# Tracing a band's combine straight behind its deformable products, with later depthwise taps tied behind its first VectorE operation

## The chip, the cores and the metric

The kernel runs on one core of a Trainium2 chip, in one launch. The metric is the device time of that launch in microseconds. A core has a matrix engine (TensorE, PE in the profile, with its weight loads as PEld), VectorE (DVE), ScalarE (ACT), GpSimd (POOL) and SyncE (SP), which run side by side, each through its own list of instructions in a fixed order, and hand results to one another by semaphores. Transfers are issued from the lists of SP, ACT and POOL.

## What is computed

Two layers over 32 images of 96 channels and 56 x 56 pixels, in float32. The first is an inverted bottleneck with a squeeze-and-excite branch, the second a block with channel and spatial attention, a plain and a deformable 3 x 3 convolution, a gate that mixes them, a normalisation over the batch, and a residual.

```
# layer 0, per image
h = silu(bn1(conv1x1(x, w1)))            # 96 -> 576 channels
h = silu(bn2(depthwise3x3(h, w2)))       # nine taps per channel
s = sigmoid(se_w2 @ silu(se_w1 @ mean(h)))
x = x + bn3(conv1x1(h * s, w3))          # 576 -> 96
# layer 1
y      = x * channel_attention(|rfft2(x)|) * spatial_attention(x)
aux    = concat(y, coords, resized mean |rfft2(y)|)
offset = conv3x3(aux, off_w)
gate   = sigmoid(dg2 @ relu(conv3x3(aux, dg1_w)))
y_base = conv3x3(y, base_w) + base_b
y_def  = einsum(bilinear samples of y at pixel + offset, def_w) + def_b
z      = (1 - gate) * y_base + gate * y_def
out    = relu(batch_norm(z over batch and pixels) + x)
```

## The kernel before

**Tiling.** An image is worked in seven bands of eight rows, 448 pixels each: 224 bands (L1088). A band is sampled in two halves h of 224 pixels. For a half, `weights_load` brings two tiles of interpolation weights, wc and wr, from memory; `weights` (L710) multiplies them on VectorE; `sample_tiles` (L739) multiplies blocks of y with the result on TensorE, in a first group of 12 matmul records and a second of 16; ScalarE copies the samples to v (L743) and packs them (L750); `deform` (L758) multiplies v with the deformable weights into the PSUM tile pd, in 14 records for a half. There is one pd buffer, shared by a band's halves, so a band's first product needs the band before to have been read out of it.

**Combining.** `combine` reads pd on VectorE in L797 (z = pd + def_b - y_base), mixes it with the gate in L798 and L799, and takes statistics of z in L800. L797 is the only reader of pd. `join` (L1063) calls `combine` and puts the store of z seven slots later.

**Three streams side by side.** While the bands of image b are sampled, the expansion and depthwise part of image b+2 (`hidden`) and the projection, transforms and attention of image b+1 (`attend`) are traced between them: `pump` (L1027) counts a slot, advances both streams in proportion, and runs what stands in the list `later` for that slot. A band has 17 slots. An image's `hidden` stream has 40 steps over 119 slots, and is started at the sixth band (j = 5, L1124). An image has nine units of hidden channels, each with nine depthwise taps on VectorE over a tile acch: the first a multiplication (L260), the other eight a multiply-add each (L262); then ScalarE applies silu (L222) and stores the unit. There are two acch and two hp buffers (hp holds the expanded channels). For the first two images alone, three of the taps run on TensorE and L258 adds them.

**What sets the order.** The order in which an engine issues is not the order of the text. A scheduler plays the program through beforehand: whenever an engine is free it takes, of the instructions whose inputs and buffers are ready in its model, the one traced first. An instruction that is traced later but ready sooner so goes ahead. On the chip that order is fixed. Three things restrain it. SP keeps the traced order (L1368). `keep_in_program_order` ties one instruction behind the instruction that was traced just before it on its engine; `weights` uses it (L710). `issue_after(i)` ties everything that a block traces on i's engine behind i. These ties are of issue order alone.

**Where the pieces are traced.** In band m, half 0: the first sampling group, three pumps, then the waiting ends: `end_half` of the band n = m - 1, half 1 (`deform` and, two slots later by way of `later`, `join`). Directly behind the ends stand `weights` for the half (m, 1) and the transposes for that half. Then come the second sampling group, four pumps and the pack. In half 1 the same is done with `end_half` of (m, 0), which has no join.

Of the kernel before, what the change touches and what calls it, by code (L numbers as in the profile page):

```python
# [1 line left out]

# [8 lines left out]
ALU = mybir.AluOpType  # L11
# [5 lines left out]
C, H, W = 96, 56, 56  # L17
# [18 lines left out]
BW = NBW  # L36
# [81 lines left out]
def bank(p):  # L118
    return p["mm"].tile([128, 512], FP, name="mm")
# [33 lines left out]
def expand(nc, p, xts, unit):  # L153


    w = p["w0"]
    ch, half = unit
    h1 = p["hp"][p["n_hp"] % len(p["hp"])]
    p["n_hp"] += 1
    p["h1"] = h1  # L160
    inv, sh = w["inv1"][:, ch : ch + 1], w["sh1"][:, ch : ch + 1]
    w1 = w["w1"][:, ch * 128 : min(HID, ch * 128 + 128)]

    def piece(parts, row0, rows):

        pt = bank(p)
        for p0, hf in parts:
            r0 = row0 - 1 + hf
            nc.tensor.matmul(pt[p0 : p0 + w1.shape[1], : rows * W], w1, xts[hf][:, r0 * W : (r0 + rows) * W],  # L169
                             start=True, stop=True)  # L170
        lo = parts[0][0]
        hi = parts[-1][0] + w1.shape[1]
        nc.scalar.activation(h1[lo:hi, row0 : row0 + rows, 1 : 1 + W],  # L173
                             pt[lo:hi, : rows * W].rearrange("p (h w) -> p h w", h=rows), AF.Silu,
                             bias=sh[lo:hi], scale=inv[lo:hi])

    if half is None:
        nc.vector.memset(h1[:64, 0, :], 0.0)
        nc.vector.memset(h1[64:, HH + 1, :], 0.0)
        for r in range(1, HH + 1, ER):  # L180
            piece([(0, 0), (64, 1)], r, ER)
            yield
        piece([(0, 0)], HH + 1, 1)
        piece([(64, 1)], 0, 1)
        yield
    else:
        r = 1 - half
        for rows in (ER + 1, ER, ER, ER):
            piece([(0, half)], r, rows)
            r += rows  # L190
            yield
# [12 lines left out]
def hidden(tc, p, x, xn, h2d, pooled, defer):  # L204


    nc = tc.nc
    w = p["w0"]

    def rows_of(x, half):  # L210
        xt = p["xt"].tile([C, (HH + 1) * W], FP, name="xt")
        r0 = half * (HH - 1)
        nc.sync.dma_start(xt, x[:, r0 : r0 + HH + 1].rearrange("c h w -> c (h w)"))
        return xt

    xts = p.pop("xts", None) or [rows_of(x, 0), rows_of(x, 1)]
    for _ in expand(nc, p, xts, UNITS[0]):
        yield
    def finish(u, acc):
        ch = UNITS[u][0]  # L220
        flat = acc.rearrange("p h w -> p (h w)")
        tc.keep_in_program_order(nc.scalar.activation(  # L222
            flat, flat, AF.Silu, bias=w["sh2"][:, ch : ch + 1], scale=w["inv2"][:, ch : ch + 1], accum_out=pooled[:, u : u + 1]))
        nc.scalar.dma_start(h2d[u], flat)

    before = None
    for u, (ch, half) in enumerate(UNITS):
        h1 = p["h1"]
        more = expand(nc, p, xts, UNITS[u + 1]) if u + 1 < len(UNITS) else iter(())
        if xn is not None and u in (5, 8):  # L230

            p.setdefault("xts", []).append(rows_of(xn, int(u == 8)))
        acc = p["acch"].tile([128, HH, W], FP, name="acch")

        rows_of_tap = lambda dy: (int(half == 0 and dy == 0), HH - int(half == 1 and dy == 2))
        diag = p.get("diag")
        taps = [k for k in (4, 0, 1, 2, 3, 5, 6, 7, 8) if diag is None or k not in TPE]
        parts = []
        if diag is not None:
            for r0 in range(0, HH, ER):  # L240
                pt = bank(p)[:, :EW].rearrange("p (h w) -> p h w", h=ER)
                for i, k in enumerate(TPE):
                    dy, dx = divmod(k, 3)
                    lo, hi = rows_of_tap(dy)
                    lo, hi = max(r0, lo), min(r0 + ER, hi)
                    nc.tensor.matmul(pt[:, lo - r0 : hi - r0], diag[:, ch, i], h1[:, dy + lo : dy + hi, dx : dx + W],
                                     start=(i == 0), stop=(i == len(TPE) - 1))
                parts.append((slice(r0, r0 + ER), pt))
            next(more, None)
            yield  # L250
        for n, k in enumerate(taps):
            dy, dx = divmod(k, 3)
            lo, hi = rows_of_tap(dy)
            win = h1[:, dy + lo : dy + hi, dx : dx + W]
            wk = w["w2"][:, ch, k : k + 1]
            if n == 0:
                for rs, pt in parts:
                    nc.vector.scalar_tensor_tensor(acc[:, rs], win[:, rs], wk, pt, ALU.mult, ALU.add)  # L258
                if not parts:
                    nc.vector.tensor_scalar(acc, win, wk, None, ALU.mult)  # L260
            else:
                nc.vector.scalar_tensor_tensor(acc[:, lo:hi], win, wk, acc[:, lo:hi], ALU.mult, ALU.add)  # L262
            if n % 2:
                if n == 3 and before:
                    finish(u - 1, before)
                next(more, None)
                yield
        for _ in more:
            pass
        before = acc  # L270
    defer(lambda: finish(len(UNITS) - 1, before))


def sigmoid(nc, out, src, bias):
# [478 lines left out]
def deform(nc, p, pd, v, h):  # L753

    out = pd[:C, :BW].rearrange("c (q w) -> c q w", q=RB)[:, :, h * W // 2 : (h + 1) * W // 2]
    for k in range(KA):
        ks = slice(0, 128 if k else C)
        nc.tensor.matmul(out.rearrange("c q (t x) -> c t q x", x=TS), p["w"]["def"][ks, k],  # L758
                         v[ks, k].rearrange("c t s (r x) -> c t (s r) x", r=TS),
                         start=(k == 0), stop=(k == KA - 1))  # L760
# [33 lines left out]
def combine(nc, p, j, pd, yb, gate, st):  # L794

    z = p["q2"].tile([C, BW], FP, name="z")
    nc.vector.scalar_tensor_tensor(z, pd[:C, :BW], p["w"]["cv"]("def_b"), yb, ALU.add, ALU.subtract)  # L797
    nc.vector.scalar_tensor_tensor(z, gate, 1.0, z, ALU.add, ALU.mult)  # L798
    nc.vector.scalar_tensor_tensor(z, z, 0.5, yb, ALU.mult, ALU.add)  # L799
    nc.vector.bn_stats(st[:, j], z)  # L800
    return z
# [152 lines left out]
def layers(tc, a, dp, x1d, zd, stats, far):  # L954
# [6 lines left out]
    nc = tc.nc  # L961
    B = x1d.shape[0]
    with ExitStack() as ctx:
        p = {"tc": tc, "dp": ctx.enter_context(tc.tile_pool(name="l1d", bufs=3, space=DRAM))}
# [11 lines left out]
        def first(b):  # L976
            if b >= B:
                return iter(())
            h2d = p["dp"].tile([len(UNITS), 128, HB], FP, name="h2d")
            pooled = p["pl"].tile([128, len(UNITS)], FP, name="pooled")  # L980
            held[b] = h2d, pooled
            return hidden(tc, p, a["x"][b], a["x"][b + 1] if b + 1 < B else None, h2d, pooled, lambda end: later.append((slot + 3, end)))
# [7 lines left out]
        streams, later = [], []  # L990
        slot = 0
# [68 lines left out]
        def store(b, j, z):  # L1060
            nc.gpsimd.dma_start(zd[b][:, j * BW : (j + 1) * BW], z)

        def join(n, pd, gate, st):  # L1063
            b, j = bands[n]
            z = combine(nc, p, j, pd, ybs[n], gate, st)
            later.append((slot + 7, lambda: store(b, j, z)))
            if j == NBD - 1:
                nc.vector.bn_aggr(stats[:, b], st)

        def end_half(n, h, v, gate, st):  # L1070
            if h == 0:
                pds[n] = p["pd"].tile([128, 512], FP, name="pd")
            deform(nc, p, pds[n], v, h)
            if h:
                pd = pds.pop(n)
                later.append((slot + 2, lambda: join(n, pd, gate, st)))

        ends, pds = [], {}

# [41 lines left out]
        for n, (b, j) in enumerate(bands):  # L1121
            if j == 0:
                st = p["st"].tile([C, NBD, 6], FP, name="st")
# [7 lines left out]
            for h in range(2):  # L1131
# [20 lines left out]
                if h == 0:  # L1152
                    if n % 2 == 0:
                        gates.extend(gates_of(nc, p, hids[n // 2]))
                    gate = gates.pop(0)
# [361 lines left out]
```

## Time and profile before

| | |
|---|---|
| median of three runs | 9030.57 us (9027.98 to 9034.88) |
| profiled execution | 9059.03 us, its span 9057.2 us |
| PE busy (matmuls) | 8175.3 us, 90% of the span |
| DVE busy | 7184.4 us, 79% |
| ACT busy | 5393.5 us, 60% |
| POOL busy | 2902.8 us, 32% |
| mean granted TensorE clock | 0.939 of full |
| depthwise multiply-adds L262 | 2250, mean 1981 ns, 4456.4 us |
| first taps L260 | 270, mean 1084 ns |
| weight products L710 | 448, mean 1265 ns |
| combine L797, L798, L799, L800 | 224 each, mean 679, 876, 679, 618 ns |
| deformable products L758 | 6272 records, 1468.8 us |

Busy time is the time in which an engine had an instruction running. A line of the waits view names an engine with the line that it wanted to run, whom it waited for, and then the total in us, how often, and the longest. A line of the timeline has the start and duration in us, engine, line, operation, written and read tiles, and how many were merged; a bracket holds the idle time just before it and what ended it. TensorE's clock is given as a share of full speed (PEclk). The last stage, the normalisation from about 8775 us on, has no matmuls.

### The profile page before, as it was taken

How to read it: one execution, taken by the hardware profiler on the slowest of the kernel's cores; microseconds unless marked ns; L12 is line 12 of the kernel's file. 1: busy time of each engine (PE TensorE's matmuls, PEld its weight loads, DVE VectorE, ACT ScalarE, POOL GpSimd, SP SyncE). 2: the span in 40 equal slices, each digit the busy share in tenths (PEclk: the TensorE clock that was granted, in tenths of full speed). 3: DMA queues.
4: the chain of work that ended last, by engine and by line, in shares of the span. 5: the costliest groups of instructions: out<-in, count | busy, mean ns of one | idle time of the engine just before them, and what ended most of it. 6: DMA issues, size and time to landing. Idle time of an engine off the chain costs nothing. (4 is left out here: it accounts for less than half of the span.)

```text
span 9057.2 us, 137476 instructions
## 1 busy us (share of the span) xinstructions
PE 8175.3 (90%) x52406; PEld 5193.5 (57%) x52406; DVE 7184.4 (79%) x6629; ACT 5393.5 (60%) x10486; POOL 2902.8 (32%) x2800
## 2 busy tenths in 40 slices
PE   5889999999999999999999999999999999999960
PEld 3456565665656566565656656565665655566640
DVE  7688888888888888888888888888888888888333
ACT  2356665666666666666666666666666666666553
POOL 0233333333333333333333333333333333333210
PEclk9889999999999999999999999999999999999985
DMA  2356666666666666666666666666666666666669
GB/s 82 108 142 160 163 169 165 157 154 153 163 166 171 166 157 147 158 165 164 172 161 154 159 157 168 165 174 161 154 154 160 165 166 172 166 156 144 144 188 416
DMA packets 1068758, 1486.48 MB, mean 164 GB/s; under 512 B 590191, under 2 KB 839839, under 8 KB 1055807
## 3 DMA queue, kind: packets, MB, share of 16 engines
q1 hardware_dynamic: 858995, 985.20, 46.4%
q10 hardware_dynamic: 153803, 329.80, 10.2%
q0 software_dynamic: 55296, 162.60, 6.7%
q8 instruction: 420, 6.88, 0.4%
q14 instruction: 244, 1.99, 0.1%
HBM read 1064.29 MB, written 412.65 MB: 163 GB/s over the span
## 5 line engine op out<-in xcount | busy, mean ns | idle before, releaser
L262 DVE SCALAR_TENSOR_TENSOR acch<-hp,w,acch 128x1512 f32<-128x1512 f32 (+1 forms) x2250 | 4456.4, 1981 | 141.4 <-ACT hp L173 103.8
L615 PE MATMUL mm<-yp,c_jointW 104*128 104x448 f32 x4032 | 1679.6, 568 | 10.1 <-DMA yp<-fqd 10.1
L758 PE MATMUL pd<-v,c_def 128*96 128x224 f32 (+1 forms) x6272 | 1468.8, 382 | 142.7 <-DVE z L797 115.6
L721 POOL COPY ybl<-yp 96x448 f32<-96x448 f32 x896 | 1048.3, 1198 | 1204.9 <-PE mm L725 1204.8
L758 PEld LDWEIGHTS pd<-v,c_def 128*96 128x96 f32 (+1 forms) x6272 | 1062.2, 176 | 449.8 <-issue 116.9
L615 PEld LDWEIGHTS mm<-yp,c_jointW 104*128 104x128 f32 x4032 | 776.6, 196 | 784.2 <-issue 747.4
L743 ACT COPY v<-mm 96x288 f32<-96x288 f32 (+1 forms) x2688 | 1004.3, 441 | 156.0 <-PE mm L739 109.3
L169 PE MATMUL mm<-xt,w 96*128 96x392 f32 (+3 forms) x2688 | 1058.5, 527 | 35.3 <-DMA xt<-in_x 33.1
L739 PE MATMUL mm<-wc,yt 64*96 64x144 f32 x12544 | 1056.9, 300 | 20.8 <-DVE sq L379 6.7
L739 PEld LDWEIGHTS mm<-wc,yt 64*96 64x96 f32 x12544 | 834.2, 164 | 317.3 <-issue 199.1
L173 ACT ACTIVATE hp<-mm,sh,inv 128x392 f32<-128x392 f32 (+2 forms) x1216 | 810.7, 673 | 344.8 <-PE mm L169 290.5
L710 DVE TENSOR_TENSOR wc<-wc,wr 128x1008 f32<-128x1008 f32 x448 | 566.6, 1265 | 412.5 <-DMA wr<-hd 385.1
L644 PE MATMUL mm<-yp,c_base0W 96*64 96x224 f32 x8064 | 830.1, 358 | 5.7 <-ACT hp L173 5.7
L329 PE MATMUL mm<-hq,w3s 128*96 128x392 f32 x2048 | 749.7, 510 | 63.6 <-DMA hq<-h2d 62.2
L672 POOL DMA_DIRECT2D od<-at x224 | 186.7, 834 | 1908.3 <-DVE at L664 1292.6
L750 ACT COPY v<-v 32x448 f32<-32x448 f32 x1344 | 755.1, 562 | 29.7
L727 ACT COPY yt<-mm 128x384 f32<-128x384 f32 (+1 forms) x896 | 353.9, 439 | 700.7 <-PE mm L725 699.0
L644 PEld LDWEIGHTS mm<-yp,c_base0W 96*64 96x64 f32 x8064 | 555.2, 135 | 282.7 <-issue 61.0
L635 ACT ACTIVATE hid<-mm,c_dg1b 50x448 f32<-50x448 f32 x224 | 140.8, 628 | 868.4 <-PE mm L615 858.4
L476 POOL TENSOR_TENSOR o<-o,xc 96x392 f32<-96x392 f32 x256 | 376.2, 1470 | 806.2 <-ACT o L339 804.2
L222 ACT ACTIVATE acch<-acch,sh,inv 128x1568 f32<-128x1568 f32 x288 | 488.4, 1696 | 202.8 <-DVE acch L262 176.5
L329 PEld LDWEIGHTS mm<-hq,w3s 128*96 128x96 f32 x2048 | 323.0, 166 | 395.2 <-issue 367.5
(194 smaller groups left out, 9325.3 us busy)
## 6 DMA issues: line engine op xcount, KB each, us to landing
h2d<-acch ACTq DMA_DIRECT2D x288, 784.0 KB
wc<-hd SPq DMA_DIRECT2D x896, 252.0 KB
wr<-hd SPq DMA_DIRECT2D x448, 504.0 KB
hq<-h2d SPq DMA_DIRECT2D x128, 980.0 KB
hq<-h2d SPq DMA_DIRECT2D x128, 784.0 KB
hq<-x1d SPq DMA_DIRECT2D x768, 98.0 KB
ht<-od SPq DMA_DIRECT2D x224, 252.0 KB
hd<-ho ACTq DMA_DIRECT2D x224, 252.0 KB
```

Of the source, the lines that this page charges most:

```text
L169: nc.tensor.matmul(pt[p0 : p0 + w1.shape[1], : rows * W], w1, xts[hf][:, r0 * W : (r0 + rows) * W], start=True, stop=True)
L173: nc.scalar.activation(h1[lo:hi, row0 : row0 + rows, 1 : 1 + W], pt[lo:hi, : rows * W].rearrange("p (h w) -> p h w", h=rows), AF.Silu, bia ...
L262: nc.vector.scalar_tensor_tensor(acc[:, lo:hi], win, wk, acc[:, lo:hi], ALU.mult, ALU.add)
L329: nc.tensor.matmul(pts[half][:C, :EW], w3s[:, ch], hq, start=(i == 0), stop=False)
L615: nc.tensor.matmul(view, weights[:, k], yp[:channels, r0 : r0 + RB, dx + PD - 1 : dx + PD - 1 + W], start=(k == 0), stop=(k == NTAP - 1))
L644: nc.tensor.matmul(pb[i * BC : (i + 1) * BC, : BW // 2].rearrange("p (h w) -> p h w", h=RB // 2), w["base"][:, k], yp[:C, r0 + i * RB // 2 ...
L710: p["tc"].keep_in_program_order(nc.vector.tensor_tensor(wc, wc, wr, ALU.mult))
L721: nc.gpsimd.tensor_copy(yb[:, :, s], blocks)
L739: nc.tensor.matmul(pt[k][:C, (t - lo) * KP : (t - lo + 1) * KP], yt[ps, t], s[ps, t * KP : (t + 1) * KP], start=True, stop=True)
L743: nc.scalar.copy(v[:C, :, lo:hi, k].rearrange("c k t p -> c t k p"), pt[k][:C, : (hi - lo) * KP].rearrange("c (t k p) -> c t k p", t=hi - ...
L750: nc.scalar.copy(v[C:, 1 + 2 * i : 3 + 2 * i], v[i * QC : (i + 1) * QC, KA:])
L758: nc.tensor.matmul(out.rearrange("c q (t x) -> c t q x", x=TS), p["w"]["def"][ks, k], v[ks, k].rearrange("c t s (r x) -> c t (s r) x", r=T ...
```

## The change

`end_half` calls `join` at once instead of putting it into `later` for two slots on. `combine` keeps its first instruction, L797, under the name "urgent". In `hidden`, every multiply-add of the depthwise part that is traced from then on is tied behind the latest such instruction. The first tap of a unit as it stands in the main loop (L260) is not inside such a block. Nothing is computed differently, and no instruction is added or removed.

```diff
@@ hidden
             if n == 0:
-                for rs, pt in parts:
-                    nc.vector.scalar_tensor_tensor(acc[:, rs], win[:, rs], wk, pt, ALU.mult, ALU.add)
+                with behind(p):
+                    for rs, pt in parts:
+                        nc.vector.scalar_tensor_tensor(acc[:, rs], win[:, rs], wk, pt, ALU.mult, ALU.add)
                 if not parts:
                     nc.vector.tensor_scalar(acc, win, wk, None, ALU.mult)
             else:
-                nc.vector.scalar_tensor_tensor(acc[:, lo:hi], win, wk, acc[:, lo:hi], ALU.mult, ALU.add)
+                with behind(p):
+                    nc.vector.scalar_tensor_tensor(acc[:, lo:hi], win, wk, acc[:, lo:hi], ALU.mult, ALU.add)
...
+def behind(p):
+    return p["tc"].issue_after(p["urgent"]) if "urgent" in p else nullcontext()
...
@@ combine
-    nc.vector.scalar_tensor_tensor(z, pd[:C, :BW], p["w"]["cv"]("def_b"), yb, ALU.add, ALU.subtract)
+    p["urgent"] = nc.vector.scalar_tensor_tensor(z, pd[:C, :BW], p["w"]["cv"]("def_b"), yb, ALU.add, ALU.subtract).ins
...
@@ end_half
-                later.append((slot + 2, lambda: join(n, pd, gate, st)))
+                join(n, pd, gate, st)
```

## The prediction

> **What bounds the kernel now.** I read the page first. TensorE is busy for 90% of the span, and in nearly all of the 40 slices for nine tenths or more; VectorE for 79%. The chain that ended last names only the closing stage without matmuls, so it says nothing of the bands.
>
> ```profile
> span 9057.2 us, 137476 instructions
> PE 8175.3 (90%) x52406; PEld 5193.5 (57%) x52406; DVE 7184.4 (79%) x6629; ACT 5393.5 (60%) x10486; POOL 2902.8 (32%) x2800
> PEclk9889999999999999999999999999999999999985
> L758 PE MATMUL pd<-v,c_def 128*96 128x224 f32 (+1 forms) x6272 | 1468.8, 382 | 142.7 <-DVE z L797 115.6
> ```
>
> So TensorE's idle time is what can be won or lost. Second, the waits of TensorE: the longest is for L797, the reader of pd; the others are small and also mostly for VectorE.
>
> ```profile
> PE pd L758 <- DVE z L797: 115.6, 26, 6.1
> PE acc L440 <- DVE m_fy L437: 72.8, 30, 5.6
> PE acc L440 <- DVE m_fe L437: 71.1, 31, 2.5
> PE mm L725 <- DVE at L664: 57.2, 28, 5.7
> ```
>
> Third, where the L797 waits lie. Over all 224 bands I took, from the instruction rows in order of time, the end of a band's last L758 record, the start of its L797 and the next L758. An idle TensorE of more than 1.5 us before that next product occurs 29 times, 124.2 us in all (the waits view puts some of it to other lines), and every one is at the last band of an image, j = 6. One of them, TensorE and then VectorE:
>
> ```profile
> 3687.09 2.81 PE L758 MATMUL pd<-v,c_def 96*96 96x224 f32 x14
> 3689.74 0.74 PE L725 MATMUL mm<-c_ident,ybl 96*128 96x96 f32 x7
> 3690.41 1.23 PE L739 MATMUL mm<-wc,yt 64*96 64x144 f32 x16
> ...
> 3693.25 0.90 PE L739 MATMUL mm<-wc,yt 64*96 64x144 f32 x12
> 3694.09 0.93 PE L169 MATMUL mm<-xt,w 96*128 96x392 f32 x2
> 3698.67 1.06 PE L758 MATMUL pd<-v,c_def 96*96 96x224 f32 x2 [3.66 <-DVE z L797]
> ...
> 3700.17 4.43 PE L758 MATMUL pd<-v,c_def 128*96 128x224 f32 x12
> ```
>
> ```profile
> 3684.42 1.19 DVE L710 TENSOR_TENSOR wc<-wc,wr 128x1008 f32<-128x1008 f32 x1
> ...
> 3691.64 6.26 DVE L262 SCALAR_TENSOR_TENSOR acch<-hp,w,acch 128x1568 f32<-128x1568 f32 x3
> 3697.94 0.68 DVE L797 SCALAR_TENSOR_TENSOR z<-pd,c_cvec,yb 96x448 f32<-96x448 f32 x1
> ```
>
> pd was done at 3689.8, three taps ran on VectorE, L797 began 8.1 us later. The product after it takes 4.43 us for 12 records against 2.81 for 14, because the clock fell:
>
> ```profile
> 3692.00:3695.00 3.00, 3.00 (x20) 1.37 (x18) 2.96 (x2) 2.98 (x6) 3.00 (x3) 1.00 0.53 157
> 3695.00:3698.70 3.70, 0.04 (x2) 0.03 (x1) 3.56 (x4) 3.63 (x8) 1.25 (x1) 0.82 0.99 300
> 3698.70:3704.80 6.10, 6.10 (x23) 4.74 (x23) 6.00 (x10) 0.84 (x2) 0.52 (x1) 0.55 1.00 226
> ```
>
> (The columns are the stretch, its length, busy time of PE, PEld, DVE, ACT, POOL, then the granted clock.) In the records of the clock, 28 of the 29 gaps are followed by a stretch at half speed, 3.4 to 10.2 us long, 211.6 us together, 43.8 of them inside the gaps; half of the other 167.8 us, 84 us, is lost.
>
> **The change, part by part.** (a) *Which taps move.* The stream of an image has 81 taps; 40 steps over 119 slots give how many are traced when the combine is traced in its new place: 33, 44, 58, 71, 0, 6, 20 for j = 0 to 6 (from j = 4 on, of the next image). The trace of before has 33, 47, 61, 73, 0, 9, 27 issued ahead of L797. So 18 taps per image run ahead of it now that could not any more, 3, 3, 2, 0, 3, 7 at j = 1 to 6 (two of them are first taps, L260, and not tied). At 1.98 us, the seven of j = 6 are 13.9 us; the delay of L797 there is 8.2 us at the median. VectorE reaches L797 about when pd is done. None of this is lost work: the taps run after L797, where VectorE has gaps (idle for 1249.8 of the 7500 us from 1000 to 8500; 4.1 us for ScalarE's hp right after L797 of j = 5).
>
> (b) *Gain.* At most 124.2 + 84 = 208 us. At least: in the gap shown TensorE fell idle at 3695.0, and ScalarE's pack of the same v (L750) ended at 3696.5, so 1.5 us of 4.28 may stay: 29 x 2.78 = 81 us. A gap of 1.5 us would be below all that lowered the clock here, so I take 81 + 84 = 165 us.
>
> The Trainium skill, "TensorE: Matmul & The Clock Gate", section "HAM oscillation — how this bites in real kernels", says that TensorE should have no idle gaps beyond about 3.4 us or the clock is halved. Gaps of 1.9 to 3.1 us did lower it here, so the rows decide; by the rule alone the clock term would be that of the 23 gaps beyond it, 67 us, and the sum below 17 us higher.
>
> (c) *What the moved join drags along.* `weights` (L710) for the half (m, 1) is tied to the instruction traced just before it on VectorE. Until now that is a piece of a stream. With `join` in front of it, it is L800 (or the aggregate behind it). So L710, which today ends 6 to 14 us before its products begin, now waits for the whole chain: pd done, L797, L798, L799, L800, L710; and the 12 products of the next half wait for that. In the trace those 12 begin 22.1, 4.7, 4.3, 7.3, 3.9, 7.7, 2.5 us after pd is done (medians, j = 0 to 6). The chain from L797's start to L800's end takes 6.5, 7.0, 8.2, 7.6, 3.3, 3.2, 3.5 us (the long ones have a tap between each two instructions), L710 1.2 us, and L797 starts 8.7, 0.7, 4.4, 7.0, 0, 0, 8.2 us after pd.
>
> From above: were TensorE's order to stay as it is, with new delays of L797 of 0, 3.7, 5, 0, 0, 0.6 at j = 1 to 6 (4.4 less the 0.7 now gone; 7.0 less that and less part of the new wait; about none where VectorE now arrives early), the waits would be 3.5, 8.8, 6.5, 0.6, 0, 2.8: 22.2 us per image, 666 us over the 30 images with such taps. From below: 0, if TensorE gets other products to do meanwhile; there are some, since the stretch after such a place is full of L169, L396 and L420. I take what no ordering beforehand can hide, because the order is fixed by a model and the chip's VectorE runs late against it: from j = 1 to j = 3 the delay of L797 grows by 7.05 - 0.72 = 6.3 us, and TensorE would have to wait that out once. For j = 1, 4 and 6 the nearest rows are TensorE's waits for m_fe (2.3 us each) and at (2.0); as there is other work to put in front I take a quarter, 0.5 us each. So 7.8 us x 30 = 234 us, and one lowered clock per image more, at 84/29 = 2.9 us: 87 us. Against it, a TensorE held up earlier is no longer early for m_fy: -73 us. Loss: 248 us.
>
> Every L262 and L710 behind a waiting L797 waits as well; VectorE is idle at L797 already 64 times, 166.1 us.
>
> (d) *Queues.* L798 to L800 and the store (L1061, on POOL, five slots behind the join as before) move up two slots. POOL waits for L799 already 203 times (520.7 us) and is 32% busy; nothing. SP's order is as traced and has no piece of this; a later L710 frees its wr buffer later, but the load that needs it is a band off; nothing, and were it not, VectorE's wait for wr (385.1 us, 113 times) would grow. The unit ended later stores later; ScalarE has 40% idle. Taken as nothing; the cover gone, it shows in L329's wait for h2d (62.2 us, 31 times).
>
> **Sum.** -165 + 248 = +83 us on the profiled 9057 us. The runs have a median of 9030.57, 28 us below the profiled execution, so I carry the difference over: 9114, rounded 9115 us.
>
> **The rivals.** *Hidden chain.* TensorE has other products for the 5 to 9 us, and VectorE, made to wait at j = 1, 5 and 6, is no longer late anywhere: then only (b) counts, 165 to 208 us, and at most 73 more. Centre 9030.6 - 165 = 8866 us, up to 9012 if some of (c) is paid. For it: the backlog at 90%, L797 as the largest wait; against it: three other VectorE results for which TensorE waits 2 us each although that order was planned too. It decides for a gain as soon as the waits of (c) stay under 165 us, 5.5 us per image. Chance 0.38. *Order as it is.* The 666 us in full, less 208: 9490 us; the place is the 12 records of L739 behind j = 2 and 3. Against it: the scheduler sees the chain. Chance 0.08. *It doesn't do what it says.* First taps and the streams' other VectorE work fill the place of the tied taps, L797 stays as late, and the chain is hidden: 9030 us. Chance 0.08. The likeliest, a loss between 9050 and 9290, has 0.46.
>
> **The numbers.** Three runs lay within 0.08%; 0.2%, 18 us, is about what a measurement can tell from no change. Slower 0.46 + 0.08 = 0.54, the same 0.08, faster 0.38. The range of the likeliest alone is 9050 to 9290; as the gain holds much of the rest, it is widened down to 8850, leaving out some 0.08 below and 0.1 above.
>
> **What would show it.** Right, if in the changed trace L797 starts within 1 us of pd at j = 6 and TensorE's wait for L797 falls under 30 us; if L710 stands behind L800 in every band; and if TensorE has a new wait of L739 for L710, today 5.2 us, above 150 us, mostly at j = 2 and 3. Wrong, if that wait stays below 50 us (the hidden chain), or if VectorE's idle time before L797, now 166 us, doesn't grow.

## The result and the profile after

The changed kernel takes 9393.77 us (median of four, 9393.22 to 9396.26) beside 9032.72 us for the kernel before, a ratio of 1.0398 (95% interval 1.038 to 1.0416): 4% slower, some 361 us. Slower was forecast, at 9115 us with an upper end of 9290; the size was missed. The profiled execution has a span of 9391.7 us, 334.5 more than before (334.5 and not 361, because the profiled execution of the kernel before took 26 us more than the median of its runs).

The same lines of the changed kernel's page, whose line numbers are a few higher (the products L739 are now L746, L758 is L765, L797 is L804, L710 is L717):

```profile
span 9391.7 us, 137436 instructions
...
PE 8329.8 (89%) x52406; PEld 5297.2 (56%) x52406; DVE 7021.2 (75%) x6629; ACT 5417.2 (58%) x10486; POOL 3257.8 (35%) x2800
...
PEclk9889999999999999999999999999999999999975
...
L746 PE MATMUL mm<-wc,yt 64*96 64x144 f32 x12544 | 1172.9, 320 | 423.1 <-issue 365.1
L765 PE MATMUL pd<-v,c_def 128*96 128x224 f32 (+1 forms) x6272 | 1407.1, 369 | 94.1 <-ACT v L757 53.2
```

TensorE has the same 52,406 records and is busy 154.5 us longer with them, since its mean clock fell from 0.939 to 0.924. Its idle time between its first and its last record (matmuls and weight loads taken together) grew from 546.9 to 723.7 us, by 176.8. Together that is 331 of the 334.5 us; the stage behind the last matmul is as long as before (289 and 290 us).

Who TensorE waited for, in the changed kernel:

```profile
PE mm L746 <- issue: 365.1, 113, 6.4
PE acc L447 <- DVE m_fe L444: 73.4, 32, 2.5
...
PE pd L765 <- DVE z L804: 37.3, 22, 6.7
...
PE acc L447 <- DVE m_fy L444: 13.4, 3, 9.1
```

The wait that was aimed at has shrunk from 115.6 to 37.3 us. A new one stands in front of the sampling products. "issue" means that the view found no releaser; the rows in order of time name it. This is the last band of an image, TensorE and then VectorE:

```profile
3787.84 2.81 PE L765 MATMUL pd<-v,c_def 96*96 96x224 f32 x14
3790.49 0.74 PE L732 MATMUL mm<-c_ident,ybl 96*128 96x96 f32 x7
3791.16 1.22 PE L746 MATMUL mm<-wc,yt 64*96 64x144 f32 x16
...
3796.09 2.51 PE L765 MATMUL pd<-v,c_def 128*96 128x224 f32 x12 [1.37 <-ACT v L757]
3802.04 1.85 PE L746 MATMUL mm<-wc,yt 64*96 64x144 f32 x12 [3.44 <-issue]
3803.82 1.68 PE L169 MATMUL mm<-xt,w 96*128 96x392 f32 x2
```

```profile
3790.69 0.68 DVE L804 SCALAR_TENSOR_TENSOR z<-pd,c_cvec,yb 96x448 f32<-96x448 f32 x1 [6.87 <-PE pd L765]
3791.30 1.78 DVE L264 SCALAR_TENSOR_TENSOR acch<-hp,w,acch 128x1512 f32<-128x1512 f32 x1
3793.00 0.97 DVE L805 SCALAR_TENSOR_TENSOR z<-gate,z 96x448 f32<-96x448 f32 x1
3793.90 1.78 DVE L264 SCALAR_TENSOR_TENSOR acch<-hp,w,acch 128x1512 f32<-128x1512 f32 x1
3795.60 0.97 DVE L806 SCALAR_TENSOR_TENSOR z<-z,yb 96x448 f32<-96x448 f32 x1
3796.49 1.84 DVE L264 SCALAR_TENSOR_TENSOR acch<-hp,w,acch 128x1568 f32<-128x1568 f32 x1
3798.26 0.61 DVE L807 BATCH_NORM_STATS2 st<-z 96x6 f32<-96x448 f32 x1
...
3800.80 2.25 DVE L717 TENSOR_TENSOR wc<-wc,wr 128x1008 f32<-128x1008 f32 x2
```

L804 now starts at the moment at which pd is done (VectorE stood idle 6.87 us for it), where it was 8.1 us late before. But a held tap slips in between each two of the combine's instructions, the weight product L717 comes last, and its first piece ends just when the 12 sampling products begin, after a wait of 3.44 us. The deformable products of the next band (L765) no longer wait for L804; the gap has moved from the one place to the other. The clock follows the gap as it did before (columns as in the same view of before):

```profile
3798.60:3802.00 3.40, 0.00 (x1) 0.00 (x0) 3.40 (x5) 0.00 (x0) 0.00 (x0) 0.90 0.93 263
3802.00:3808.50 6.50, 6.46 (x38) 5.03 (x38) 6.50 (x6) 3.10 (x7) 1.75 (x2) 0.53 0.92 155
```

Before, one such gap per image; now four, at j = 2, 3, 5 and 6. From the instruction rows, medians over images 2 to 28 (counted from 0), and the mean of the new gap:

| j of the combined band | 0 | 1 | 2 | 3 | 4 | 5 | 6 |
|---|---|---|---|---|---|---|---|
| first combine instruction after pd, before -> after, us | 8.4 -> 6.6 | 0.7 -> 0 | 4.4 -> 0 | 7.0 -> 2.1 | 0 -> 0 | 0 -> 0 | 8.2 -> 0 |
| combine's four instructions take, before -> after | 7.7 -> 5.3 | 7.0 -> 6.3 | 8.2 -> 8.7 | 7.6 -> 7.5 | 3.3 -> 3.3 | 3.2 -> 8.3 | 3.5 -> 8.2 |
| sampling products after pd, before -> after | 21.7 -> 22.1 | 4.7 -> 7.9 | 4.3 -> 9.9 | 7.3 -> 10.9 | 3.9 -> 4.9 | 7.7 -> 10.4 | 2.5 -> 11.4 |
| weight product's end to those products, after | 8.6 | 0.7 | 0.1 | 0.1 | 0.5 | 0.1 | 0.1 |
| new gap of TensorE there, mean | 0 | 0 | 2.75 | 3.57 | 0 | 2.51 | 3.33 |

At j = 0 odd and even images differ so much that one median says little (in the changed kernel the first combine instruction comes 1.8 us after pd in the odd ones and 7.3 in the even ones); that is also why the prediction has 8.7 and 6.5 us there for the kernel before and this table 8.4 and 7.7.

### The profile page after: what moved, and what is told of

Same layout as the page of the kernel before. It is cut to its first block, busy times and chain, and to the rows that moved or that the text cites. A ratio compares the mean times of both kernels' runs of the same rounds, so it can differ in the third digit from the quotient of the medians.

```text
span 9391.7 us, 137436 instructions
## 1 busy us (share of the span) xinstructions
PE 8329.8 (89%) x52406; PEld 5297.2 (56%) x52406; DVE 7021.2 (75%) x6629; ACT 5417.2 (58%) x10486; POOL 3257.8 (35%) x2800
## 5 line engine op out<-in xcount | busy, mean ns | idle before, releaser
L264 DVE SCALAR_TENSOR_TENSOR acch<-hp,w,acch 128x1512 f32<-128x1512 f32 (+1 forms) x2250 | 4263.8, 1895 | 114.7 <-ACT hp L173 87.4
L728 POOL COPY ybl<-yp 96x448 f32<-96x448 f32 x896 | 1508.7, 1710 | 2323.4 <-PE mm L732 2323.3
L746 PE MATMUL mm<-wc,yt 64*96 64x144 f32 x12544 | 1172.9, 320 | 423.1 <-issue 365.1
L765 PE MATMUL pd<-v,c_def 128*96 128x224 f32 (+1 forms) x6272 | 1407.1, 369 | 94.1 <-ACT v L757 53.2
L746 PEld LDWEIGHTS mm<-wc,yt 64*96 64x96 f32 x12544 | 914.8, 177 | 721.1 <-issue 577.3
L765 PEld LDWEIGHTS pd<-v,c_def 128*96 128x96 f32 (+1 forms) x6272 | 1020.7, 170 | 414.9 <-issue 129.9
L169 PE MATMUL mm<-xt,w 96*128 96x392 f32 (+3 forms) x2688 | 1103.0, 545 | 34.1 <-DMA xt<-in_x 33.2
L336 PE MATMUL mm<-hq,w3s 128*96 128x392 f32 x2048 | 772.0, 522 | 7.5 <-DMA hq<-h2d 5.9
L804 DVE SCALAR_TENSOR_TENSOR z<-pd,c_cvec,yb 96x448 f32<-96x448 f32 x224 | 152.1, 679 | 804.2 <-PE pd L765 803.0
L717 DVE TENSOR_TENSOR wc<-wc,wr 128x1008 f32<-128x1008 f32 x448 | 576.8, 1292 | 234.2 <-DMA wr<-hd 224.2
L169 PEld LDWEIGHTS mm<-xt,w 96*128 96x128 f32 (+1 forms) x2688 | 373.0, 183 | 333.1 <-issue 183.8
```

The lines of the kernel that those rows point to most:

```text
L336: nc.tensor.matmul(pts[half][:C, :EW], w3s[:, ch], hq, start=(i == 0), stop=False)
L717: p["tc"].keep_in_program_order(nc.vector.tensor_tensor(wc, wc, wr, ALU.mult))
L728: nc.gpsimd.tensor_copy(yb[:, :, s], blocks)
L746: nc.tensor.matmul(pt[k][:C, (t - lo) * KP : (t - lo + 1) * KP], yt[ps, t], s[ps, t * KP : (t + 1) * KP], start=True, stop=True)
```

## The experiments

The theory, C: the time goes into the chain deformable products, four combine instructions, weight product, next sampling products, which the moved join made by standing in front of the weight product's tie. The rival, H: it goes into the taps held behind the first combine instruction; VectorE waits there 803 us in the changed kernel, 166 before. For each run the ratio to the kernel before on the same chip is given with its 95% interval, and TensorE's idle time in front of the sampling products (20.8 us before, 419.0 in the changed kernel) and in front of the deformable ones (142.2 and 93.4).

| run | chain | taps tied at | ratio (interval) | median us | idle before sampling | idle before deformable |
|---|---|---|---|---|---|---|
| changed kernel | full | all bands | 1.0398 (1.038 to 1.0416) | 9393.77 | 419.0 | 93.4 |
| e1 | none | all bands | 0.9962 (0.9945 to 0.998) | 9022.43 | 101.9 | 61.7 |
| e2 | full | none | 1.0788 (1.0769 to 1.0807) | 9769.54 | 546.5 | 99.5 |
| e3, late join | none | all bands | 0.9928 (0.9912 to 0.9945) | 8981.18 | 72.7 | 29.2 |
| e4 | full | all, behind the last instruction | 1.0684 (1.0666 to 1.0701) | 9672.06 | 582.2 | 43.7 |
| e5 | first instruction only | all bands | 1.0106 (1.0084 to 1.0128) | 9128.83 | 141.8 | 14.6 |
| e6, late join | none | last band | 0.9972 (0.9955 to 0.9988) | 9005.19 | 64.2 | 22.6 |
| e7 | none | last band | 0.9994 (0.9981 to 1.0006) | 9038.31 | 104.8 | 48.9 |
| e8 | none | none | 1.0008 (0.9997 to 1.0019) | 9049.15 | 29.0 | 170.0 |
| e9 | full, kept free | all, and other work | 1.0353 (1.0326 to 1.0379) | 9343.21 | 190.6 | 30.5 |

**The chain removed (e1).** In the changed kernel the weight product is traced ahead of the waiting ends:

```diff
+                        ready.extend(weights(nc, p, *ws) for ws in loads[:1])
+                        del loads[:1]
                         for end in ends:
                             end()
                         ends.clear()
...
-                        ready.extend(weights(nc, p, *ws) for ws in loads[:1])
-                        del loads[:1]
```

> The change with one move: in the waiting ends' place, the weight product for the next half is traced ahead of the ends instead of behind them, so its tie is again to a stream instruction and not to the combine's last one. Theory C (the chain from the deformable products through the four combine instructions and the weight product to the next 12 sampling products costs the time): TensorE's gaps before the sampling products, 419 us in the changed kernel, fall under 60 us, and the time comes to 8850 to 8960 us. Rival H (the taps held behind the first combine instruction cost it: VectorE stands 803 us at that instruction): the taps are still held, so 9250 us or more, and the gaps move to other lines.

9022.43 us: this one move takes away 4.4% of the time before (0.9962 against 1.0398), with every tap still tied and VectorE still waiting 472.9 us for pd (803.0 in the changed kernel):

```profile
DVE z L804 <- PE pd L765: 472.9, 142, 8.4
...
PE mm L746 <- DVE sq L386: 80.1, 31, 3.4
```

H, which asked for 9250 us or more, falls. Both sizes of C were missed: 9022, not 8960 us or less, and 101.9 us of idle time, not under 60, since 77 us of it turned up behind the combine of j = 0, a place where the changed kernel had 11.

**The early combine without ties (e2).** `behind` does nothing:

```diff
-    return p["tc"].issue_after(p["urgent"]) if "urgent" in p else nullcontext()
+    return nullcontext()
```

> The combine is traced directly behind the products as in the change, but no tap is tied. Theory C: the weight product still stands behind the combine, which now starts later because taps run ahead of it again, so the gaps before the sampling products stay, 300 us or more, and the time is 9250 us or more. Rival H: without the held taps the time is back at 9030 us or below.

9769.54 us, 7.9% slower than before; the changed kernel's 4.0% has nearly doubled (1.0788 against 1.0398). C's sizes hold and H's 9030 us doesn't. Without ties L804 comes late again at some bands (6.3 us after pd at j = 6) and the weight product with it. More is lost at j = 2 (222.8 us of idle time before the sampling products, 92.3 in the changed kernel): there the attention product L609 comes to stand in the chain and waits for its load 30 times, 107.6 us in all. At j = 5 the chain takes 3.2 us again, as in the kernel before, and the gap is gone (2.5 us in all, 75.2 in the changed kernel). On balance the ties soften the loss.

**The ties without the early combine (e3).** As the change, with the old line in `end_half`:

```diff
-                join(n, pd, gate, st)
+                later.append((slot + 2, lambda: join(n, pd, gate, st)))
```

> The taps are tied behind the first combine instruction as in the change, but the combine is traced two slots later as before, so the weight product is traced ahead of it. Theory C: no chain; TensorE's gap at the last band of an image (124 us and 84 us of clock) goes too, time 8850 to 8980 us. Rival H: 9250 us or more.

8981.18 us, 0.7% faster than before (0.9928, 0.9912 to 0.9945): by its median the fastest kernel of the study, though 1 us above C's range; H falls again. L804 starts with pd at j = 6, the gap in front of the deformable products falls from 142.2 to 29.2 us, and the weight product stands behind a combine's last instruction in 2 of 223 bands, as in the kernel before.

**The ties moved to the last combine instruction (e4).** "urgent" is the statistics instruction, so no tap can slip into the chain:

```diff
-    p["urgent"] = nc.vector.scalar_tensor_tensor(z, pd[:C, :BW], ..., ALU.subtract).ins
+    nc.vector.scalar_tensor_tensor(z, pd[:C, :BW], ..., ALU.subtract)
...
-    nc.vector.bn_stats(st[:, j], z)
+    p["urgent"] = nc.vector.bn_stats(st[:, j], z).ins
```

> The change, with the taps tied behind the combine's last instruction (statistics) instead of its first. Theory C, with the length of the chain as the size: without taps between its four instructions the chain takes 3.3 us instead of 8.3 in every band, the weight product ends about 4.6 us after pd instead of 7.5 to 11, the gaps before the sampling products fall from 419 to under 120 us and the time to 8900 to 9050 us. If the length doesn't matter and any tie of the weight product to the combine costs: 9300 us or more. Rival H: taps are held longer still, so above 9394 us.

9672.06 us, 6.8% slower: C's expectation failed, and the time alone would suit H (above 9394 us) or a tie that costs whatever its length. The rows tell otherwise. The taps are out of the chain at most bands, but at j = 2 and 6 other work moved into their places. VectorE, at j = 2:

```profile
4008.67 0.68 DVE L804 SCALAR_TENSOR_TENSOR z<-pd,c_cvec,yb 96x448 f32<-96x448 f32 x1 [3.28 <-PE pd L765]
4018.91 0.68 DVE L609 SCALAR_TENSOR_TENSOR yp<-yp,ca,sab 96x448 f32<-96x448 f32 x1 [9.56 <-DMA yp<-x1d]
4019.52 0.61 DVE L805 SCALAR_TENSOR_TENSOR z<-gate,z 96x448 f32<-96x448 f32 x1
...
4021.84 1.19 DVE L717 TENSOR_TENSOR wc<-wc,wr 128x1008 f32<-128x1008 f32 x1
```

The attention product L609 stands between the first and second instruction and waits 9.56 us for its load; all behind it wait too, and TensorE waits 10.13 us for its sampling products there. At j = 6 a channel sum waiting for a load does the same (6.10 us). Over the run these waits inside the chain come to 277.6 us at j = 2 and 98.4 us at j = 6. Where nothing took the taps' place, at j = 5, the chain takes 3.2 us and the gap is gone (2.6 us in all, 75.2 in the changed kernel), as C has it.

**The chain cut to one instruction (e5).** The weight product is traced between the combine's first and second instruction:

```diff
 def combine(nc, p, j, pd, yb, gate, st):
...
+    p.pop("between", lambda: None)()
     nc.vector.scalar_tensor_tensor(z, gate, 1.0, z, ALU.add, ALU.mult)
...
+                        def product():
+                            ready.extend(weights(nc, p, *ws) for ws in loads[:1])
+                            del loads[:1]
+                        p["between"] = product
                         for end in ends:
                             end()
...
```

> The change with the weight product traced between the combine's first and second instruction, so that it is tied to the combine, but to its first instruction alone. Theory C with the chain's length as the size: the product ends within 2 to 4 us of pd, mostly before the 12 sampling products were due (2.5 to 7.7 us in the kernel before), so TensorE's gaps before them, 419 us in the changed kernel, fall under 120 us and the time to 8980 to 9080 us. If any tie of the weight product to the combine costs as much: gaps over 300 us and 9300 us or more.

9128.83 us: the weight product ends 1.8 us after pd at most bands (3.0 and 4.1 at j = 4 and 3), the idle time falls from 419.0 to 141.8 us. Both expected sizes were missed by a little, the direction is C's: what counts is how long the chain is, not that there is a tie. Some 1.4% more than e1 is left; at each j = 3 there is still a gap of 1.75 us.

**Ties at the last band alone**, with the late join (e6) and with the weight product ahead (e7):

```diff
-    p["urgent"] = nc.vector.scalar_tensor_tensor(z, pd[:C, :BW], ..., ALU.subtract).ins
+    first = nc.vector.scalar_tensor_tensor(z, pd[:C, :BW], ..., ALU.subtract).ins
+    if j == NBD - 1:
+        p["urgent"] = first
```

> The combine traced two slots later as before, and taps tied behind the first combine instruction of an image's last band alone, where the kernel before had TensorE's gaps. Theory D: holding taps at the other bands only makes VectorE idle and gives part of the gain back; then this is below the 8981 us of the ties at all bands, 8870 to 8960 us, with the gap at the last band gone. If the ties at the other bands do no harm: 8980 us or more.

> The change with the weight product traced ahead of the ends, and taps tied at an image's last band alone. Theory D: below the 9022 us of the same with ties at all bands, 8900 to 8990 us. Otherwise 9020 us or more.

9005.19 and 9038.31 us: theory D, that ties are of use only at the last band and do harm at the others, falls twice. The ties at the other bands do no harm; e3 and e1, which have them, are a little faster.

**The early combine alone (e8)**, without chain and ties: the move of e1 and the edit of e2 together.

> The combine traced directly behind the products, the weight product ahead of both, no tap tied: the early combine alone, without chain and without ties. Theory C: no new gaps before the sampling products (under 60 us), the gap at the last band stays, 9000 to 9070 us. If the early combine costs by itself: 9150 us or more.

9049.15 us, 1.0008: nothing, as C expected. It completes a square of four, all with the early combine: no chain and no ties 1.0008, ties 0.9962, chain 1.0788, both 1.0398. The chain costs 7.8% without ties and 4.4% with them.

e7 against e8 also shows what the gap at the last band is worth: the same kernel but for ties at that band. TensorE's waits in e8, then in e7:

```profile
PE pd L765 <- DVE z L804: 134.2, 31, 10.3
PE acc L447 <- DVE m_fy L444: 71.6, 31, 5.9
```

```profile
PE mm L746 <- DVE sq L386: 83.8, 31, 5.3
PE acc L447 <- DVE m_fe L444: 72.1, 31, 3.0
```

134.2 us of waiting for L804 are gone and 83.8 us of waiting for the channel sums L386 have come. The taps held back at the last band run just when VectorE has these sums to do; the sums read PSUM banks, and the sampling products want the banks (e10 to e12 test that). Whether e7 is any faster than e8 the intervals don't tell: 0.9981 to 1.0006 and 0.9997 to 1.0019.

**The chain kept free (e9).** As e4, with L609 and the channel sums tied behind the last combine instruction too:

```diff
+    with behind(p):
+        nc.vector.scalar_tensor_tensor(rows, rows, p["ca", b], sab, ALU.mult, ALU.mult)
...
+            with behind(p):
+                nc.vector.tensor_reduce(parts[:, k, g], t.rearrange("h c w -> h w c"), AX.X, ALU.add)
```

> The change with everything that filled the combine's chain tied behind its last instruction: the taps (L264), the attention product (L609) and the channel sums (L386). Theory C, length of the chain: 3.3 us in every band, the weight product ends about 4.5 us after pd, TensorE's gaps before the sampling products (419 us in the changed kernel, 582 us with only the taps behind the last instruction) fall under 150 us, most of it at the last band; 9020 to 9150 us. If it is the tie to the combine and not the chain's length: above 9390 us.

The chain takes 3.3 us or less at all bands but j = 0, and the idle time before the sampling products falls from 582.2 (e4) to 190.6 us (under 150 was expected). That much of C holds. The time, 9343.21 us, doesn't follow, and lies between the ranges of C and of its alternative: TensorE is now idle for 161.2 us in front of L169 (before: 35.2) and 111.6 in front of the projection L336 (before: 62.7).

```profile
PE mm L169 <- ACT yt L736: 113.1, 29, 6.1
PE mm L336 <- DMA hq<-h2d: 110.3, 31, 4.9
```

Tying more work behind the combine moved the wait. That the sums and the taps held back make ScalarE's copies yt and the loads of h2d late is likely, but no run shows it.

**The squares in SBUF.** The channel sums read their squares from a buffer of an existing pool instead of a PSUM bank, in e3 (e10), in the kernel before (e11), and in e7 (e12):

```diff
-        sq = bank(p)[: 2 * H, : CG * W].rearrange("h (c w) -> h c w", c=CG)
+        sq = p["sq"].tile([2 * WX, 2, NPB * V], FP, name="sq")[: 2 * H, 0, : CG * W].rearrange("h (c w) -> h c w", c=CG)
```

> Combine two slots later, taps tied at all bands (8981 us), and the squares for the channel sums written to SBUF instead of a PSUM bank (one buffer of an existing pool; the numbers are the same). Theory E: part of the gain is given back one band later, where the sampling products wait for PSUM banks that the late sums hold (53 us there now); without that wait 8890 to 8950 us. If the wait only moves on: 8970 us or more.

> The kernel before with the same squares in SBUF. Theory E: there the sampling products waited for these banks 5 us in all, so the time is within 0.3% of before, 9015 to 9065 us. If the move of the squares is a gain by itself: below 9000 us.

> Combine traced directly, weight product ahead of it, taps tied at the last band alone (9038 us), with the squares in SBUF. Theory E: the 79 us of waits at the first band go, with the clock that they cost: 8910 to 8980 us. If the wait only moves on: 9020 us or more.

8982.65 us (0.9948, 0.9931 to 0.9966), 9061.67 (1.003, 1.0014 to 1.0045) and 9101.46 (1.007, 1.0052 to 1.0088). The idle time before the sampling products is 58.5, 61.2 and 63.0 us, before the deformable ones 62.0, 89.0 and 62.9. Theory E's times held in e11 alone; in e10 and e12 its alternative came true, that the wait only moves on. The waits behind j = 0 are gone in e10 and e12 (from 53.0 to 2.9 and from 81.2 to 7.5 us), but no time is won, and e12 is slower than e7. The waits have moved: 39 and 41 us stand before the sampling products at j = 6 instead, in e12 the idle time before m_fe's products grew from 71.2 to 122.2 us and that before L169 from 50.6 to 78.7, and in e10 the deformable products wait for ScalarE's copies of the samples:

```profile
PE pd L765 <- ACT v L750: 60.5, 50, 5.3
```

Theory E, that the channel sums' hold on the banks eats the gain, names a real wait, but not one that holds the gain back by itself. The edit is no clean test either: it changes the order that the scheduler makes (in e11 the sampling products behind j = 0 begin 7.1 us after pd, 21.7 in the kernel before).

## Why the prediction was right or wrong

**Right.** The mechanism of (c): the moved join puts the combine in front of the weight product's tie. Its signs were named: L717 behind L807 (in 214 of 223 bands, where it was 2), a new wait before the sampling products above 150 us (it is 419.0, at j = 2, 3, 5, 6), L804 within 1 us of pd at j = 6, VectorE idle for longer before it (803.0 us, 166.1 before). Two signs held in part: TensorE's wait for L804 fell to 37.3 us, not under 30, and nearly half of the new wait is at j = 5 and 6, not mostly at j = 2 and 3. The count of taps in (a) held too: from j = 5 over j = 0 to j = 3, 6, 20, 30 or 32, 45, 58 and 72 are issued ahead of the first combine instruction (6, 20, 33, 44, 58 and 71 were forecast). e1 and e3, with e2 and e8 beside them, show that this, and not the held taps, costs the time. The sign and the likeliest case's mechanism held.

**Wrong: the size of the loss, in three terms.** What failed first is the 234 us taken for the new waits, and with it the +3 us of clock. The sum had 234 us of new waits before the sampling products, +3 us of clock (87 less 84), -73 of m_fy, -81 of gap: +83. Measured between the two profiled executions (+334.5 us):

- The waits before the sampling products are 419.0 - 20.8 = 398 us. The step that failed is the split by bands. I took one wait of 6.3 us for the lateness of the first combine instruction at j = 2 and 3, half a microsecond at j = 1, 4 and 6, and nothing at j = 5. Lateness has little to do with it: the first combine instruction starts with pd at j = 2, 5 and 6, and 2.1 us behind it at j = 3. The chain itself is too long, and it is longer than I took it at j = 5 and 6: 8.3 and 8.2 us, not 3.2 and 3.5, because the taps that the change holds back are just there to slip in (in e2, without ties, it takes 3.2 and 3.3 us at j = 5 and 6). I carried the chains of before over into a kernel whose first effect is to put taps behind L804. Gaps of 2.5 to 3.6 us at four bands make 12.2 us per image, not 7.8. The upper end, 22.2 us with TensorE's order kept, allowed for it; TensorE did find other products (at j = 6 the sampling products moved from 2.5 to 11.4 us after pd), but not enough.
- The clock: 132 gaps of over 1 us before the sampling products are followed by 100 stretches at half speed, some three per image instead of one more. TensorE is busy 154.5 us longer for the same records. Counting half of the recorded half-speed time outside gaps gives 351.7 us before and 479.7 after, +128 us, against +3 in the sum. The prediction also took a gap of 1.5 us as shorter than all that lowered the clock; the trace of before has three gaps of 1.20 us in front of L758, each followed within 0.4 us by 3.4 us at half speed.
- The gain, 165 us, was too large, and only part of it came: the idle time before the deformable products fell by 49 us, since at j = 6 those for the next half now wait for ScalarE's pack (1.37 us in the rows above, the lower bound's 1.5). Where the chain is absent, most of that idle time goes (170.0 us in e8, 48.9 in e7), and yet e7 gains nothing measurable over e8, and e3, the best, 0.7% over before. What I had priced as time won was a wait that other results, some microseconds later, take over.

The credits went the other way: m_fy fell by 60 us (73 taken), the transposes' wait for L664 by 57 and the projection's for its load by 55 us, which I had at nothing; a TensorE that is held up is probably no longer early for them. 398 + 128 - 49 - 60 - 57 - 55 = 305 us, of 334.5; the rest is mostly busy time that the count of half-speed stretches doesn't cover (128 of 154.5 us). The 112 us of credits that I had left out hide part of the miss.

**The rivals.** "Order as it is" lies nearest, 9490 us against 9394, but by luck: of its 666 us of waits 398 came, it had no loss of clock (+128 us), and it took the whole 208 us as won. It named two of the four places. "Hidden chain" is false for the change; without its chain (e1, e3) the gain that it promised, 165 us or more, isn't there either.

**Not settled.** Whether TensorE had products ready to put into the 2.5 to 3.6 us gaps wasn't tried. Why so little of the gain at the last band is left even without the chain is known only as far as the waits that came up elsewhere; no run frees them all.

## What to carry to other kernels

An instruction that is tied to "whatever was traced just before it" changes its meaning when something is traced in between: before a step is moved, look for such ties directly behind the new place, and count the whole chain that they then close, with what can slip between its links in the new order, not in the old. Holding work back behind a waiting instruction frees that instruction, but the work held back is late for someone: the gain to expect is the wait less the next one, and here that was about a third of it at best (e3: 65 of the 165 to 208 us). If such a tie pays (e3), put the early step where no other tie hangs on it.

## What the runs showed that was not expected

A short gap of TensorE is paid for twice: in the kernel before, 29 gaps of 124 us together cost some 84 us more in clock, and in the changed kernel 132 gaps before the sampling products (409 us) were followed by 100 half-speed stretches, 621 us together. And on VectorE's list an open place between two dependent instructions is dangerous by what fills it: a tap costs 1.8 us (changed kernel), an instruction that waits for a load cost 9.56 us (e4), and the waiting engine was TensorE, 10.13 us.
